# A graph layer on one core: fourteen blocks of nodes gathered, not twelve, through five message tiles

## The chip, the cores and the metric

The kernel runs on one core of a Trainium2 chip. The metric is the device time of one execution in microseconds; lower is better. The kernel before was timed three times: 592.69, 594.62 and 597.58 us, so 594.62 us is its median.

The core's engines work side by side, each on its own queue of instructions, which it takes strictly in order: PE (matrix products), DVE or VectorE, ACT or ScalarE, POOL or GpSimd, and SP, which here only starts transfers. `T`, `V`, `A` and `G` are PE, VectorE, ScalarE and GpSimd in the code.

## The reference

There are 6250 nodes with 128 features each and 100,000 edges, sorted by the node that they point to. An edge has a source, a destination and a type, 0 or 1. The layer computes, for every edge, a linear map of the source's features with the weights of its type, sums these messages at the destination, adds a linear map of the node itself, applies relu, adds the input and normalises each row:

```python
Xs = X[src]
m_data = Xs @ W_data.T + b_data
m_ctrl = Xs @ W_control.T + b_control
msg = jnp.where((edge_types == 0)[:, None], m_data, m_ctrl)
agg = jax.ops.segment_sum(msg, dst, num_segments=X.shape[0])
out = agg + (X @ W_self.T + b_self)
return _layernorm(x + jax.nn.relu(out))
```

The last line joins two lines of the reference. Everything is float32.

## The kernel before

**The table.** The kernel first maps every node with both sets of weights: 49 blocks of 128 nodes, two types, so 98 sub-blocks of 128 rows. Each float32 result is split into three bfloat16 parts that add up to it, so a row has 3 x 128 = 384 numbers. All rows lie in SBUF (`m3`) and also go to DRAM (`table`). The products are `y` at L460 and L462; L478 subtracts the part already taken. The table's stores (L488) are issued by SP.

**A block's edges.** Because edges are sorted, the edges into one block of 128 destinations lie together. The kernel loads for each block a window of 128 x 18 edges (`win` or `win_g`, L372) that covers them. From there, a block takes one of two ways.

**The gathered way** (the last `NG` blocks). For each of a window's 18 columns, POOL starts an indirect transfer that fetches 128 rows of the table from DRAM into a tile `msg` (L854, 98 KB). VectorE writes a matrix of zeros and ones that says which destination each edge has (`hot_g`, L866, six columns at a time), and PE multiplies the two into the sum of the block (`agg_g`). That is 18 steps, and each is four products, since `by_columns` (L232) splits a product into four column pieces of 32 that run side by side. The tiles `msg` are `MB` in number, so gather `i` waits for the product `i - MB` (the step `gm`).

**The packed way** (the first `NPB` blocks). It fetches nothing by row from DRAM. For groups of four or five blocks (`GROUPS`) PE and VectorE sort the edges by the sub-block that their source lies in. Ranking does that: `acc` products with `tri` and `rest` and a reduction `slot` (L563) for each of the 18 columns. The sorted entries are moved to their slots by small products (`small`, L600), written to DRAM (`packed`, L618), and read back spread over all partitions (`rows`, 784 KB for a block, L718). Edges that found no slot go to a list of up to 32, fetched by one indirect transfer per group (`mixed`, L694). Then, for each block, PE picks message rows out of `m3` with `rows` as selecting matrix (`g_ps`, L754, 98 products of 32 rows each, in 25 tiles), ACT copies each tile from PSUM to SBUF (`gs`, L769), and PE adds them up with `hot_d` (L739) into `agg`, four column pieces for each of 25 tiles. In the last group VectorE shares the copies with ACT.

Both ways end alike: the node's own product (`o`), the sum of the three parts (`whole`, L153), relu and residual (L149), the statistics, and once per batch of blocks the normalisation (L168 to L190) and the store. A batch is a group on the packed way, with the last group in two pieces; on the gathered way it is `GQ` blocks.

**What sets the order.** Every part of the work is written as a stream of steps, each with a cost per engine, the steps that it needs, and a due time. A planner (`Order.run`, from L76) takes all streams together and simulates the engines with these costs: it picks the engine that is free first, and of the steps that it could begin, the one with the earliest due time. The order in which it picks them is the order of the instructions in each engine's queue. The costs and due times are numbers in the program, no measurements: `BUILT` is when the table is due, `BLOCK` the time of one packed block, `PACE` that of one gather, `AHEAD` how far ahead of its first block a group's packing is due, and `FIRST` the same for the first group. `PACE` is also the cost of a gather on POOL in the plan, and a gather is planned to land 3.0 us after it starts. On the chip the engines wait for one another by semaphores, so the plan decides the order and not the times.

The part of the plan that the change touches is this:

```python
free = [("gm", *gathered[i - MB])] if i >= MB else [*stored, "idx"]
yield step(("msg", j, k), {"G": PACE}, *free, lag=3.0 - PACE)
msgs[j, k] = late.tile([P, D3], BF16, name="msg", bufs=MB)
```

`stored` are all stores of the table: no gather starts before the whole table is in DRAM.

Of the kernel before, what the change touches and what calls it, by code (L numbers as in the profile page):

```python
# [32 lines left out]
ES = ER // RJ  # L33
EPS = 1e-05

GROUPS = (4,)*2+(5,)*5+(4,)
Q = max(GROUPS)
NPG = len(GROUPS)
NPB = sum(GROUPS)
NG = NB - NPB  # L40
STARTS = [sum(GROUPS[:i]) for i in range(NPG)]
R = 32
# [58 lines left out]
def step(name, costs, *needs, lag=0.0):  # L101
    return as_tuple(name), costs, [as_tuple(n) for n in needs], lag
# [7 lines left out]
def kernel(  # L110
# [95 lines left out]
    with ExitStack() as main:  # L206
        sums_over_windows(main, tc, x, xt, edges, w, bias, table, packed, total,
                          add_parts, finish, load_rows, norm)
# [6 lines left out]
def sums_over_windows(ctx, tc, x, xt, edges, w, bias, table, packed, total,  # L215
# [67 lines left out]
    for j in range(RJ):  # L283
# [17 lines left out]
    counted = {n: const.tile([P, P, n], BF16, name=f"count{n}")  # L301
               for n in sorted({DC, CH, *GROUPS})}
    tri = const.tile([P, P], BF16, name="tri")
# [5 lines left out]
    slot_values = [const.tile([P, (Q + 1) // 2, NT], BF16, name=f"vs{i}") for i in range(2)]  # L309
    slot_b = {n: const.tile([P, R, n], BF16, name=f"slot{n}") for n in sorted({*GROUPS})}  # L310

# [68 lines left out]
                  for g, n in enumerate(PARTS) for b in range(at_part[g], at_part[g] + n, 2)]  # L380


    LEAD, BUILT = 8.0, 78
    BLOCK = 12.9
    PACE = 2.2
    AHEAD, FIRST = 22.0, 14

    def due(kind, *i):
        if kind in ("p", "g") and i[0] in ("root", "rooted", "scale", "apply", "out"):
            n = i[1] + 1  # L390
            return BUILT + 10 + (BLOCK * sum(p[2] for p in PIECES[:n]) if kind == "p" else PACE * KT * GQ * n)
        if kind in ("counted", "turned", "first"):
# [21 lines left out]
        if kind in ("win", "xs", "agg", "o", "whole", "sum"):  # L414
            b = i[0]
            begun = BUILT + (BLOCK * b if b < NPB else PACE * KT * (b - NPB))
            if kind == "win":
                return due("fields", blocks[b][0]) - 8 if b < NPB else BUILT - 20
            if b >= NPB:
                return begun + {"whole": PACE * KT + 2, "sum": PACE * KT + 5}.get(kind, 0)  # L420
            return begun + {"whole": BLOCK + 0.5, "sum": BLOCK + 3}.get(kind, 0.3 * BLOCK)
        if kind in ("rows", "sel", "d", "g", "e", "s"):
            of = {"rows": 1, "sel": 1, "d": 2}.get(kind, NS)
            lead = {"rows": -9, "sel": -3, "d": -1, "g": 0, "e": 1, "s": 2}[kind]
            return BUILT + BLOCK * (i[0] + (i[1] / of if len(i) > 1 else 0)) + lead
        if kind in ("gh", "gm", "msg"):
            k = i[1] * CH if kind == "gh" else i[1]
            return BUILT + PACE * (i[0] * KT + k) + {"msg": 0, "gh": 2, "gm": 5}[kind]
        n = GROUPS[i[0]]
        end = BUILT + BLOCK * STARTS[i[0]] - (AHEAD if i[0] else FIRST)  # L430
        span = BLOCK * n if i[0] else 34.0
        begun = end - span
# [399 lines left out]
    rel_g = const.tile([P, NG, KT], BF16, name="rel_g")  # L832
    msgs, g_hots, kept = {}, {}, []
    GQ = -(-NG // -(-NG // Q))
    MB, XB = 3, 2

    def gathered_fields():
        yield step("idx", {"V": 1.8}, ("y", NB * 3 // 4), *[("win", b) for b in range(NPB, NB)])
# [10 lines left out]
    def gather_rows():  # L849
        for i, (j, k) in enumerate(gathered):  # L850
# [3 lines that stand above are left out]
# [190 lines left out]
```

## Time and profile before

| | before |
|---|---|
| median of three runs | 594.62 us |
| the profiled execution's own time | 628.32 us |
| its span, first to last instruction | 626.6 us |
| PE busy | 554.5 us (88%) |
| ACT busy | 448.4 us (72%) |
| DVE busy | 448.2 us (72%) |
| POOL busy | 255.6 us (41%) |
| moved by DMA | 77.37 MB, 123 GB/s |
| packed blocks, gathered blocks | 37, 12 |

The profile is one execution with the recorder on, and it takes 5.7% longer than the median of the runs without it. Times inside it are set against its own 628.32 us. In it the table is built in the first 75 us or so; then packed and gathered blocks run interleaved until about 603 us, the last gathered block is finished, and the last stores go out. A name such as `g_ps<-m,rows` reads: output tile from input tiles. Matmuls overlap in PE, so the durations of a group add up to more than its busy time. PEld is PE's loading of weights, which runs beside the products.

### The profile page before, as it was taken

To read this page: it belongs to the slowest core of one execution; us is meant where nothing else is said; L and a number is where in the kernel's file an instruction comes from. 1 tells how busy PE (TensorE), PEld (TensorE's weight loads), DVE (VectorE), ACT (ScalarE), POOL (GpSimd) and SP (SyncE) were. 2 spreads that over 40 slices of the span, in tenths; PEclk is the share of its full clock that TensorE was granted. 3 is DMA by queue.
4 is the path that set the end of the run, shared out by engine and by line. 5 is a ranking of instruction groups with operands and counts; after the bars stand their busy time and mean duration, and the time that the engine had idled before them with its cause. 6 is when DMAs were issued, how large, how long until landed. Compare 5 with 4: busy or idle time off the path is not lost.

```text
span 626.6 us, 27468 instructions
## 1 busy us (share of the span) xinstructions
PE 554.5 (88%) x11703; PEld 453.8 (72%) x11703; DVE 448.2 (72%) x1031; ACT 448.4 (72%) x1066; POOL 255.6 (41%) x232
## 2 busy tenths in 40 slices
PE   5899879999999989899999989999998899998950
PEld 3555447887887778787887877788886788777730
DVE  4645687897888786688768876788857766568650
ACT  6756546768877767688678768778787887777631
POOL 1000025544545445545455345455435444444330
PEclk9999989999999999999999999999999999999985
DMA  3669653243434442444324433434424443533120
GB/s 106 187 170 273 203 198 111 53 157 107 136 121 149 118 116 61 153 123 133 106 61 160 125 104 110 146 121 127 129 56 155 135 123 103 158 102 119 45 58 21
DMA packets 59642, 77.37 MB, mean 123 GB/s; under 512 B 15344, under 2 KB 50395, under 8 KB 59511
## 3 DMA queue, kind: packets, MB, share of 16 engines
q1 hardware_dynamic: 47653, 50.56, 25.4%
q0 software_dynamic: 10704, 21.56, 12.5%
q10 hardware_dynamic: 1154, 3.41, 1.8%
q8 instruction: 93, 1.52, 1.0%
q14 instruction: 38, 0.31, 0.2%
HBM read 62.44 MB, written 13.07 MB: 120 GB/s over the span
## 4 chain that ended last, share of the span: by engine, by line
PE 73%; DMA 9%; DVE 5%; issue 5%; ACT 4%; POOL 1%; SPq 1%; another core or an unknown queue 0%; ACTq 0%; POOLq 0%; DVEq 0%
PE agg L232 25%; PE g_ps L754 23%; PE acc L232 8%; DMA msg<-table,idx 7%; PE agg_g L232 6%; PE small L600 5%; PE y L460 3%; ACT gs L769 2%; PE y L478 1%; POOL msg L854 1%; DVE slot L563 1%; ACT h_p L190 1%; DMA rows<-packed 1%; PE y L462 1%; DVE two L584 1%
## 5 line engine op out<-in xcount | busy, mean ns | idle before, releaser
L769 ACT CAST gs<-g_ps 128x384 bf16<-128x384 f32 x856 | 357.8, 494 | 120.8 <-PE g_ps L754 85.7
L754 PE MATMUL g_ps<-m,rows 128*32 128x384 bf16 x3626 | 347.7, 332 | 6.2 <-issue 2.9
L854 POOL DMA_INDIRECT msg<-table,idx x216 | 243.4, 1127 | 263.6 <-PE agg_g L232 122.7
L232 PE MATMUL agg<-gs,hot_d 128*32 128x384 bf16 x3552 | 321.9, 334 | 16.7 <-ACT gs L769 8.2
L232 PEld LDWEIGHTS <-hot_d 128*32 128x32 bf16 x3700 | 212.5, 137 | 47.1 <-issue 36.3
L754 PEld LDWEIGHTS <-rows 128*32 128x32 bf16 x3626 | 201.4, 138 | 31.2 <-issue 25.6
L563 DVE TENSOR_REDUCE slot<-acc 128x5 bf16<-128x490 f32 (+1 forms) x144 | 90.2, 627 | 76.2 <-PE acc L232 49.8
L232 PE MATMUL agg_g<-msg,hot_g 128*32 128x384 bf16 x864 | 93.7, 333 | 13.5 <-DMA msg<-table,idx 11.2
L739 DVE TENSOR_TENSOR hot_d<-count,to 128x1664 bf16<-128x1664 bf16 x74 | 78.7, 1066 | 10.8 <-ACT to L634 5.1
L600 PE MATMUL small<-hot_st,two 128*32 128x98 bf16 x1332 | 66.2, 283 | 2.3 <-DVE ls L684 1.5
L232 PE MATMUL acc<-hot_st,tri 128*32 128x490 bf16 (+1 forms) x576 | 65.4, 359 | 0.2 <-issue 0.2
L232 PE MATMUL acc<-hot_st,rest 128*32 128x490 bf16 (+1 forms) x544 | 60.1, 361 | 6.2 <-DVE slot L563 5.6
L232 PEld LDWEIGHTS <-hot_g 128*32 128x32 bf16 x864 | 46.0, 124 | 19.5 <-issue 18.1
L471 ACT CAST m<-y 128x512 bf16<-128x512 f32 (+1 forms) x75 | 40.9, 580 | 25.9 <-PE y L462 12.8
L600 PEld LDWEIGHTS <-two 128*32 128x32 bf16 x1332 | 53.9, 116 | 6.5 <-issue 2.9
L546 DVE TENSOR_TENSOR hot_st<-count,st_b 128x2940 bf16<-128x2940 bf16 (+1 forms) x24 | 45.0, 1880 | 13.5 <-PE small L600 9.7
L694 POOL DMA_INDIRECT mixed<-table,row_i x8 | 9.9, 1234 | 83.2 <-DVE rows L725 79.0
L725 DVE TENSOR_SCALAR rows<-rows,pid 128x3136 bf16<-128x3136 bf16 x37 | 38.6, 1042 | 2.8 <-DMA rows<-packed 2.3
L460 PE MATMUL y<-w_sb,xt 128*128 128x256 f32 x98 | 34.4, 438 | 1.8 <-DMA xt<-in_xt 1.8
L232 PEld LDWEIGHTS <-rest 128*32 128x32 bf16 x544 | 24.1, 98 | 15.1 <-issue 14.3
L153 DVE TENSOR_REDUCE whole<-agg 128x128 f32<-128x384 f32 x37 | 20.5, 553 | 11.2 <-PE agg L232 5.6
L769 DVE CAST gs<-g_ps 128x384 bf16<-128x384 f32 x32 | 17.2, 555 | 15.2 <-PE g_ps L754 14.4
(140 smaller groups left out, 440.6 us busy)
## 6 DMA issues: line engine op xcount, KB each, us to landing
rows<-packed SPq DMA_DIRECT2D x37, 784.0 KB
table<-m SPq DMA_DIRECT2D x10, 768.0 KB
msg<-table,idx POOLq DMA_INDIRECT x216
xt<-in_xt ACTq DMA_DIRECT2D x5, 512.0 KB
xt_p<-in_xt SPq DMA_DIRECT2D x37, 64.0 KB
xs_p<-in_x SPq DMA_DIRECT2D x37, 64.0 KB
out<-h_p SPq DMA_DIRECT2D x5, 320.0 KB
win<-in_edges SPq DMA_DIRECT2D x37, 27.0 KB
```

Of the source, the lines that this page charges most:

```text
L153: nc.vector.tensor_reduce(whole, agg.rearrange("p (i c) -> p c i", i=3), axis=AX.X, op=ALU.add)
L232: T.matmul(out[c : c + 32], lhsT[:, c : c + 32], rhs, **flags)
L460: T.matmul(y[:, j, :], xts[g][:, b + j - at_part[g], :], w_sb[:, : 2 * D], start=j == 0, stop=False, skip_group_check=True)
L471: A.copy(part_of(b, n, i), ys[b][:, :n, :].rearrange("p b (t c) -> p t b c", t=2))
L546: V.tensor_tensor(hot, counted[n][:, None, 1 : NT + 1, :].to_broadcast([P, KC, NT, n]), fields[grp][2][:, c * KC : c * KC + KC, None, :].t ...
L563: V.tensor_reduce(slots[grp][:, k, :], by_q, axis=AX.X, op=ALU.max)
L600: T.matmul(vt[c0 : c0 + R, q // 2, :], two[:, k % KC, i, :, q], hot[:, k % KC, :, q], start=k == 0 and q < 2, stop=k == KT - 1, skip_group ...
L725: V.tensor_scalar(rows[b], rows[b], pid1, None, op0=ALU.is_equal)
L739: V.tensor_tensor(hot, counted[DC][:, :, :n], places[grp][:, q, None, c * DC : c * DC + n].to_broadcast([P, P, n]), op=ALU.is_equal)
L754: T.matmul(g_ps[t * R : (t + 1) * R, :D3], rows[b][:, :, s], m3[:, s, :], start=True, stop=True)
L769: (A.copy if e == "A" else V.tensor_copy)(gs[at], g_tiles.pop((b, g))[at, :D3])
L854: G.indirect_dma_start(out=msgs[j, k], out_offset=None, in_=table[:, :], in_offset=bass.IndirectOffsetOnAxis(ap=idx[:, j, k : k + 1], axis=0),
```

## The change

Three things change, all of them numbers.

- `GROUPS` goes from two groups of four, five of five and one of four (37 blocks) to seven of five (35 blocks). The number of gathered blocks, `NG`, is what is left of 49: 12 becomes 14, with 18 gathers each, so 216 gathers become 252. `GQ`, the batch of gathered blocks that are normalised together, goes from 4 to 5 by its formula, so the batches are 5, 5 and 4.
- The plan's numbers: `BUILT` 78 to 76, `BLOCK` 12.9 to 13.1, `PACE` 2.2 to 1.75, `AHEAD` 22 to 26, `FIRST` 14 to 20.
- `MB`, the number of tiles for gathered messages, goes from 3 to 5.

```diff
-GROUPS = (4,)*2+(5,)*5+(4,)
+GROUPS = (5,)*7
...
-    LEAD, BUILT = 8.0, 78
-    BLOCK = 12.9
-    PACE = 2.2
-    AHEAD, FIRST = 22.0, 14
+    LEAD, BUILT = 8.0, 76
+    BLOCK = 13.1
+    PACE = 1.75
+    AHEAD, FIRST = 26.0, 20
...
-    MB, XB = 3, 2
+    MB, XB = 5, 2
```

Since the planner orders all queues together, the order of instructions shifts on every engine from the first group on; no instruction of a new kind appears.

## The prediction

> **What bounds the kernel now.** First the page's busy times, with the rows of PE and POOL in the view of the span in 40 slices (one slice is 15.7 us):
>
> ```profile
> PE 554.5 (88%) x11703; PEld 453.8 (72%) x11703; DVE 448.2 (72%) x1031; ACT 448.4 (72%) x1066; POOL 255.6 (41%) x232
> ...
> PE   5899879999999989899999989999998899998950
> ...
> POOL 1000025544545445545455345455435444444330
> ```
>
> PE is at eight tenths or more nearly everywhere between the third slice and the last two; summed in stretches of 20 us from 100 to 600 us its busy time is 93% of the 500 us. No other engine is near that. POOL, which only issues gathers, is half busy. So work taken from PE should count nearly in full, and POOL has room. Next the costliest groups (busy us, mean ns of one, then idle time before them and who ended it):
>
> ```profile
> L769 ACT CAST gs<-g_ps 128x384 bf16<-128x384 f32 x856 | 357.8, 494 | 120.8 <-PE g_ps L754 85.7
> L754 PE MATMUL g_ps<-m,rows 128*32 128x384 bf16 x3626 | 347.7, 332 | 6.2 <-issue 2.9
> L854 POOL DMA_INDIRECT msg<-table,idx x216 | 243.4, 1127 | 263.6 <-PE agg_g L232 122.7
> L232 PE MATMUL agg<-gs,hot_d 128*32 128x384 bf16 x3552 | 321.9, 334 | 16.7 <-ACT gs L769 8.2
> L232 PE MATMUL agg_g<-msg,hot_g 128*32 128x384 bf16 x864 | 93.7, 333 | 13.5 <-DMA msg<-table,idx 11.2
> ```
>
> ACT waits for PE (85.7 us), PE hardly for ACT (8.2 us). POOL stood idle 263.6 us before gathers, because a tile of messages was not free. PE lost 11.2 us waiting for messages to land. The table of waits says it from both ends (us in total, times, longest):
>
> ```profile
> POOL msg L854 <- PE agg_g L232: 122.7, 78, 3.8
> POOL msg L854 <- PE g_ps L754: 107.0, 96, 4.1
> ...
> PE agg_g L232 <- DMA msg<-table,idx: 11.2, 10, 2.4
> ```
>
> Then prices. Matmuls overlap, so their 332 ns are not what one costs PE; the chain that ended last shows the pace at which it advances (start, us, what):
>
> ```profile
> 169.97 0.21 PE acc L232 x4
> 170.17 0.16 PE agg L232 x4
> ...
> 188.67 0.33 PE agg L232 x8
> ```
>
> Four column pieces of 384 take 0.163 us (0.33 over two such fours); four of 490 take 0.21 us. The same chain has 1.84 us for 49 `small` matmuls, 0.0376 us each, and 0.17 us for four `acc` pieces of a group of four (392 wide). Last, the end of the chain:
>
> ```profile
> 601.59 0.75 PE g_ps L754 x2
> ...
> 603.28 0.35 PE agg_g L232 x8
> ...
> 606.23 2.68 DMA msg<-table,idx
> ...
> 608.95 0.60 PE agg_g L232 x3
> ```
>
> The packed work is done at 603.3; the last six steps of the gathered blocks still follow, the last three at the pace of POOL's gathers (603.72, 604.98, 606.23, so 1.26 us apart). The last product ends at 609.55.
>
> **What the Trainium skill says.** "TensorE: Matmul & The Clock Gate", section Back-to-back issue gap, gives an isolated gap of N / 2.4 + 2.5 ns, 162.5 ns for 384 columns and 207 ns for 490; this trace agrees (163 and 210 ns for a four, whose pieces run side by side). "DMA: Bandwidth & Descriptors", section Anatomy of one DMA, fits 2.0 us plus bytes over 436 GB/s to a DMA from GpSimd, for 98 KB an estimate of 2.2 us; the last gather's 2.68 us above, undisturbed by other gathers' waits, is near, while in mid-run the chain shows 4.8 to 7.7 us. "SBUF — State Buffer", its box on how DVE blocks such DMAs, says that descriptor writing stops while VectorE holds the shared port; gathers that took POOL from 0.94 to 2.53 us fit, but no run here isolates it. So landing is a matter of latency, which more tiles in flight cover, unless the transfers themselves are the limit.
>
> **The change part by part.** All in the profile's own time: span 626.6, program 628.32 us; the median of the runs shown is 594.62, a factor of 0.946, by which I scale a difference.
>
> *Two blocks leave the packed path.* Each has 98 `g_ps` and 100 `agg` pieces: 396 pieces, 99 fours at 0.163: -16.1 us of PE. *They join the gathered path*: 2 x 18 fours of `agg_g`: +5.9. Their own-row products (`o`) stay. *Packing* goes from three groups of four and five of five to seven of five. Ranking has 35 fours a group: before 105 x 0.17 + 175 x 0.21 = 54.6, after 245 x 0.21 = 51.5: -3.1. `small` at L600 loses 72 x 0.0376: -2.7. One group's list and position products and two blocks' transposes (L629: 3.5 us for 148) go: about -0.4. Sum on PE: **-16.4 us**, on the path, since PE sets it. That PE's 7% of idle time shrinks with the work would add 1 to 3 us; I take nothing for it and keep 3 for the range.
>
> *Work on engines with room.* ACT loses 50 evictions x 0.42 (357.8 / 856), 21 us; VectorE two `rows` (1.04), four `hot_d` (1.07) and packing, and gains six `hot_g` (0.55): about -10 us net. SP loses two `rows` transfers of 784 KB and one group's stores. POOL gains 36 gathers x 1.127 = 40.6 us and loses one `mixed` (1.2). None counts: PE's queue hides them. Were POOL alone the limit, 252 gathers at the 1.25 us of back-to-back ones are 315 us, well under the 520 from first to last gather. In the last group VectorE shares the evictions over five blocks, not four; also hidden.
>
> *Five tiles.* A gather waits for the product five places back, not three. At before's mean pace, (606.2 - 87.3) / 215 = 2.41 us, three tiles are a ring of 7.2 us, and landings of 4.8 to 7.7 us stall PE. At a needed pace of some 1.95 us (490 / 252) five tiles are a ring of 9.8 us. Three at that pace would be 5.9 us, so the closer pace needs the tiles. PE's waits for messages are 11.2 us, of which 2.28 + 0.76 + 0.73 = 3.8 at the end; from the 7.4 in mid-run I take back **3 us** (bounds: none, as landings lengthen, and all 7.4). What is late next there is PE's wait for evictions (8.2 us), which is small.
>
> *The end.* In the instruction order of the changed program PE's last gathered four stands 6.5 fours of `g_ps` and 10 of `agg` ahead of its end (2.7 us), where before six gathered fours followed all else. The run then ends with the last packed block, which before had finished at 603.3, against 609.55: **-6 us** (bounds 0, if PE waits for messages there as before, and -7). The last gathered batch stays four blocks (batches of 5, 5, 4), and its 5 us of normalising run beside the last products.
>
> *The start.* The first group has five blocks: in the order, PE's work ahead of the first `g_ps` (a `y` product by the chain at 0.43, 0.21 and 0.11 us for L460, L462 and L478) is 59.8 us against 58.3 (inside the sum above). But the first group's transposes now stand 6.7 us of work ahead of the last table product, not 0.7 us; before, the last `y` ended at 73.8 and the first `g_ps` began only at 82.6, behind VectorE's list and select. That may give up to 4 us. Against it: SP's queue now has the first group's stores and three `rows` spreads ahead of the last four table stores, where one pair of stores was ahead of all of that and two spreads stood ahead of the last pair. One more 784 KB at the 220 GB/s of 60 to 80 us is 3.6 us later for the table and so for the first gather (before at 87.3); PE comes to its first message 10.2 us of work after the first `g_ps` instead of 6.7, which covers that. I take 0, bounds -4 and +5.
>
> *Plan numbers* (`BUILT`, `BLOCK`, `PACE`, `AHEAD`, `FIRST`) only reorder the queues; no wait is added. A message not landed holds everything behind it on PE: `g_ps`, then ACT's evictions. `XB` stays 2; a chunk of hots lasts six steps, 11.7 us, so its 0.55 us stays hidden.
>
> Sum: -16.4 - 3 - 6 + 0 = -25.4: 628.3 becomes 602.9, and x 0.946 is **570.5 us**.
>
> **The rivals.** *PE work only*: landings lengthen with five in flight, and the end keeps a wait. Then only -16.4 stays: 611.9, or 579. For it: waits for messages came in bursts in mid-run; against: POOL's stalls were for tiles. *Slower: gathers set the pace.* If before's spacing was the transfers' own and not the three tiles', 36 more gathers lengthen the run. The point is a mean pace of (609.55 - 87.3) / 252 = 2.07 us; at 2.15 the last gather lands near 629, 20 us late: about 648, or 613. For it: landings of up to 7.7 us and the mean of 2.41. Against: POOL waited on PE in 174 of the spaced gathers, and the last ones landed 1.26 us apart. *It does little*: later table stores hold PE at its first message and new in-order stalls cost 20 us more: about 589 to 600; the 3.6 us above speaks against that much. *More*: idle shrinks with the work, all mid-run waits go, and the start gains 4: -37, some 560.
>
> **How the numbers follow.** Forecast (562 to 577) 0.60; PE only (577 to 588) 0.20; more (under 562) 0.07; little (589 to 600) 0.06; slower 0.07. About 1%, 6 us, is what a measurement of this kernel can tell from no change. The range of 560 to 588 leaves out the little and slower cases and the far end of the best. Faster 0.87, same 0.06, slower 0.07.
>
> **What would show it.** Right: 3430 `g_ps`, 1008 `agg_g` pieces; PE busy near 538; POOL's idle before gathers down by more than half of 263.6; mean gather spacing near 1.95 us; PE's wait for messages under 8 us; the chain ending in `h_p` or only just in `h_g`, with no string of message waits at the end. Wrong: message waits above 15 us on PE, a mean spacing over 2.07 us, or a first `g_ps` later than 87 us.

## The result and the profile after

The changed kernel takes 547.74 us, the median of four runs (545.63 to 548.73). Four runs of the kernel before, on the same chip, have a median of 593.65 us (590.95 to 597.58). The ratio is 0.9217, with a 95% interval of 0.9157 to 0.9277, so the change saves 46 us. The forecast was 570.5 us, a saving of 24. The direction was right; the time lies 12 us below the low end of the range.

One fact has to come first, because the comparisons below depend on it. The experiments ran on five chips, each in one session, and the kernel before falls into one of two groups by chip. On chips 1, 8 and 14 its median is 592 to 597 us, as in the result above. On chips 13 and 15 the very same program takes 626 us, and no session mixes the two. As each chip had one session only, "chip" here may stand for something else that was the same throughout it. The profile that the prediction was read from took 628.32 us itself, beside runs of 592.69 to 597.58 us, so it looks like an execution of the second group (no chip is recorded with it). Below, "595-us chip" and "626-us chip" name the two groups, and every ratio is to the kernel before on the same chip. The ratios leave out runs that lie more than 1.5% above the fastest of the same kernel.

The busy times of the changed kernel, and the rows of PE and POOL in the view of the span in 40 slices (13.6 us each):

```profile
span 543.9 us, 26402 instructions
...
PE 504.0 (93%) x11222; PEld 440.7 (81%) x11222; DVE 425.9 (78%) x958; ACT 422.6 (78%) x1012; POOL 296.4 (54%) x267
...
PE   4899978999899999999999999999999999979990
...
POOL 1000004776766667767487576676677556676610
```

The profiled execution took 545.63 us, one of the four runs of the median, with no 5.7% on top. PE was busy 504.0 us where I had foreseen about 538, from a profile in which the kernel before has 554.5; on chip 1 it has 528.2. From the twelfth slice to the 35th every digit of PE is 9. The costliest groups, and the waits (total us, times, longest):

```profile
L769 ACT CAST gs<-g_ps 128x384 bf16<-128x384 f32 x807 | 334.3, 495 | 71.3 <-PE g_ps L754 58.2
L854 POOL DMA_INDIRECT msg<-table,idx x252 | 285.9, 1135 | 133.7 <-PE g_ps L754 64.9
L754 PE MATMUL g_ps<-m,rows 128*32 128x384 bf16 x3430 | 319.1, 331 | 0.0
L232 PE MATMUL agg_g<-msg,hot_g 128*32 128x384 bf16 x1008 | 108.0, 329 | 7.2 <-DMA msg<-table,idx 6.8
```

```profile
POOL msg L854 <- PE g_ps L754: 64.9, 121, 2.6
...
POOL msg L854 <- PE agg_g L232: 50.3, 75, 2.7
...
PE agg_g L232 <- DMA msg<-table,idx: 6.8, 8, 1.6
```

The counts are the foreseen ones. POOL's idle time before gathers fell from 263.6 us in the first profile (230.8 on chip 1) to 133.7, and PE waits 6.8 us for messages. The gathers start from 89.0 to 520.4 us, so their mean spacing is 431.4 / 251 = 1.72 us, where before it was 2.41. The end of the chain (start, us, what):

```profile
530.36 1.02 PE agg L232 x14
531.38 0.54 DVE whole L153
...
533.04 1.65 ACT h_g L190 x4
...
535.97 0.49 ACT h_p L190
```

The last product belongs to a packed block, at 531.4 us; the last product of messages began at 527.3. There is no string of waits for messages at the end, and `h_p` is the last to be normalised.

### The profile page after: what moved, and what is told of

It is laid out like the page before. It is cut to its first block, busy times and chain, and to the rows that moved or that the text cites. A ratio compares the mean times of both kernels' runs of the same rounds, so it can differ in the third digit from the quotient of the medians.

```text
span 543.9 us, 26402 instructions
## 1 busy us (share of the span) xinstructions
PE 504.0 (93%) x11222; PEld 440.7 (81%) x11222; DVE 425.9 (78%) x958; ACT 422.6 (78%) x1012; POOL 296.4 (54%) x267
## 4 chain that ended last, share of the span: by engine, by line
PE 72%; DMA 11%; DVE 9%; ACT 3%; issue 2%; SPq 1%; POOL 1%; DVEq 0%; ACTq 0%; POOLq 0%
PE agg L232 23%; PE g_ps L754 22%; PE acc L232 8%; PE small L600 7%; PE agg_g L232 7%; DMA msg<-table,idx 5%; DMA rows<-packed 5%; PE y L460 2%; DVE hot_st L546 2%; DVE slot L563 1%; ACT gs L769 1%; ACT h_p L190 1%; PE y L478 1%; DVE rows L725 1%; ACT h_g L190 1%
## 5 line engine op out<-in xcount | busy, mean ns | idle before, releaser
L769 ACT CAST gs<-g_ps 128x384 bf16<-128x384 f32 x807 | 334.3, 495 | 71.3 <-PE g_ps L754 58.2
L854 POOL DMA_INDIRECT msg<-table,idx x252 | 285.9, 1135 | 133.7 <-PE g_ps L754 64.9
L754 PE MATMUL g_ps<-m,rows 128*32 128x384 bf16 x3430 | 319.1, 331 | 0.0
L232 PE MATMUL agg<-gs,hot_d 128*32 128x384 bf16 x3360 | 298.2, 329 | 3.7 <-ACT gs L769 3.2
L232 PEld LDWEIGHTS <-hot_d 128*32 128x32 bf16 x3500 | 188.8, 137 | 11.4 <-issue 6.8
L232 PE MATMUL agg_g<-msg,hot_g 128*32 128x384 bf16 x1008 | 108.0, 329 | 7.2 <-DMA msg<-table,idx 6.8
L563 DVE TENSOR_REDUCE slot<-acc 128x5 bf16<-128x490 f32 x126 | 83.5, 663 | 36.3 <-PE acc L232 28.3
L232 PE MATMUL acc<-hot_st,rest 128*32 128x490 bf16 x476 | 54.4, 376 | 7.9 <-DVE slot L563 7.8
L232 PE MATMUL acc<-hot_st,tri 128*32 128x490 bf16 x504 | 60.5, 375 | 1.1 <-DVE hot_st L546 1.1
L694 POOL DMA_INDIRECT mixed<-table,row_i x7 | 8.2, 1169 | 86.5 <-PE g_ps L754 80.5
L546 DVE TENSOR_TENSOR hot_st<-count,st_b 128x2940 bf16<-128x2940 bf16 x21 | 41.9, 1999 | 7.7 <-PE small L600 6.3
L153 DVE TENSOR_REDUCE whole<-agg 128x128 f32<-128x384 f32 x35 | 19.3, 552 | 12.3 <-PE agg L232 9.2
L769 DVE CAST gs<-g_ps 128x384 bf16<-128x384 f32 x33 | 18.0, 555 | 12.9 <-PE g_ps L754 12.4
```

Of the source, the lines that this page charges most:

```text
L153: nc.vector.tensor_reduce(whole, agg.rearrange("p (i c) -> p c i", i=3), axis=AX.X, op=ALU.add)
L232: T.matmul(out[c : c + 32], lhsT[:, c : c + 32], rhs, **flags)
L546: V.tensor_tensor(hot, counted[n][:, None, 1 : NT + 1, :].to_broadcast([P, KC, NT, n]), fields[grp][2][:, c * KC : c * KC + KC, None, :].t ...
L563: V.tensor_reduce(slots[grp][:, k, :], by_q, axis=AX.X, op=ALU.max)
L754: T.matmul(g_ps[t * R : (t + 1) * R, :D3], rows[b][:, :, s], m3[:, s, :], start=True, stop=True)
L769: (A.copy if e == "A" else V.tensor_copy)(gs[at], g_tiles.pop((b, g))[at, :D3])
```

## The experiments

The theories have letters, and the expectations use them. **A**: the ring of three message tiles cost PE far more than the 11.2 us that the profile before names. **B**: it cost what that profile names, and the rest comes from the new order. **C**: the gain beyond the tiles comes from the plan's numbers. **D**: a plan in which the gathers end long before the packed work fills PE badly. **E**: the next bound is the pace of POOL or of the transfers, near 1.5 us. **F**: on a 626-us chip PE has stalls of its own, which the tiles do not touch.

### The parts one by one, on chip 14

The kernel before takes 596.74 us here. The first kernel keeps before's order of instructions on every engine and gives the messages five tiles. The planner still believes in three, because only the pool's size is changed:

```diff
-            msgs[j, k] = late.tile([P, D3], BF16, name="msg", bufs=MB)
+            msgs[j, k] = late.tile([P, D3], BF16, name="msg", bufs=5)
```

> The kernel before with every instruction in the order that it had, and five tiles behind msg where it had three. Theory A (the ring of three tiles cost PE far more than the 11.2 us that the profile names, since a late message also holds the copies and the weight loads behind it): 20 to 30 us faster, 565 to 575 us, PE's idle time before weight loads falls by half. Theory B (the ring costs what the profile names, the rest of the gain is the new plan of the order): 3 to 7 us faster, 587 to 591.

The second is its mirror image, the changed kernel's order with three tiles:

```diff
-            msgs[j, k] = late.tile([P, D3], BF16, name="msg", bufs=MB)
+            msgs[j, k] = late.tile([P, D3], BF16, name="msg", bufs=3)
```

> The changed kernel with every instruction in its order, but three tiles behind msg. Theory A: the gain goes, 575 to 600 us, mean gather spacing over 1.9 us and messages late on PE by 20 us or more in all. Theory B: 551 to 556 us, a loss of 4 to 8 us.

The third and fourth take one part each, the groups or the plan's numbers, with three tiles:

```diff
-GROUPS = (4,)*2+(5,)*5+(4,)
+GROUPS = (5,)*7
```

> The kernel before with seven groups of five, so fourteen gathered blocks, its old plan numbers and three tiles. PE has 16.4 us less to do by the prediction's prices. Theory A: the ring of three tiles has 36 more gathers to serve at 2.2 us of plan, which ends them after the packed work: no gain or slower, 590 to 610. Theory B: about 16 us faster, 577 to 582.

```diff
-    LEAD, BUILT = 8.0, 78
-    BLOCK = 12.9
-    PACE = 2.2
-    AHEAD, FIRST = 22.0, 14
+    LEAD, BUILT = 8.0, 76
+    BLOCK = 13.1
+    PACE = 1.75
+    AHEAD, FIRST = 26.0, 20
```

> The kernel before with the new plan numbers (BUILT, BLOCK, PACE, AHEAD, FIRST) only: 37 packed blocks, three tiles. Theory A: the closer pace asks three tiles for what they cannot give, so within 5 us of before or slower, 589 to 610. Theory B: 10 to 20 us faster, 574 to 584, from the earlier start and the gathers that end before the packed work.

| part of the change | us | ratio to before (95%) | PE's wait for messages, us |
|---|---|---|---|
| before's order, five tiles | 569.69 | 0.956 (0.950 to 0.962) | 5.1 |
| the new order, three tiles | 609.59 | 1.022 (1.014 to 1.031) | 61.2 |
| groups alone, three tiles | 628.51 | 1.055 (1.050 to 1.061) | 53.7 |
| plan's numbers alone, three tiles | 629.76 | 1.053 (1.044 to 1.062) | 48.6 |

The 609.59 us is the middle of 606.47 and 612.71; the other two runs of that kernel took 628.63 and 615.75 us, and the last is the profiled one. Five tiles alone, in an unchanged order, save 27.0 us. Everything else without them makes the kernel slower by 2 to 5%, and PE waits 49 to 61 us for messages. The table of waits of the new order with three tiles:

```profile
PEld L232 <- issue: 97.5, 108, 4.7
...
PE agg_g L232 <- DMA msg<-table,idx: 61.2, 52, 4.5
```

The changed kernel has 6.8 us there, in the same order with two tiles more. This speaks for A in its direction, and it shows that the closer pace needs the tiles. The sizes are beyond A: it gave the three kernels without the tiles at most 600, 610 and 610 us. But 27 us is more than the 11.2 us of the profile before, all of it; why is answered below by a profile of before taken on a 595-us chip.

### The parts in pairs and a step further, on chip 13

Here the kernel before was also run by itself once more:

> The kernel before, unchanged. Its first profile took 628.32 us, 33 us over its median, while the changed kernel's profile took what its median says. If recording slows a kernel whose queue waits on three tiles, this profile takes 615 us or more again; if that execution was an odd one, 590 to 602.

Then the changed kernel with the old groups (12 gathered blocks), and with the old plan's numbers:

```diff
-GROUPS = (5,)*7
+GROUPS = (4,)*2+(5,)*5+(4,)
```

> Five tiles and the new plan numbers, but the old groups (37 packed blocks, 12 gathered). Theory A (with the ring gone, PE's work sets the time): the two blocks are worth the 16.4 us of PE's priced work, so 561 to 567 us. Rival C (the gain past the five tiles is the plan numbers'): 548 to 555. Rival D (gathers planned at 1.75 end far ahead of 37 packed blocks, so PE is less well filled late): 568 to 580.

```diff
-    LEAD, BUILT = 8.0, 76
-    BLOCK = 13.1
-    PACE = 1.75
-    AHEAD, FIRST = 26.0, 20
+    LEAD, BUILT = 8.0, 78
+    BLOCK = 12.9
+    PACE = 2.2
+    AHEAD, FIRST = 22.0, 14
```

> Five tiles and seven groups of five, but the old plan numbers, so gathers planned 2.2 us apart: 252 of them end about 554 in the plan, after the packed work at 78 + 35 x 12.9 = 530. Theory A: the two blocks' work goes from PE, but the last gathered blocks are left alone at the end: 560 to 575 us. Rival C: like the same-order run with five tiles, 566 to 572, as only the plan numbers would help. Were the plan numbers worth nothing: 546 to 552.

And a step further on the same way, with 17 blocks gathered:

```diff
-GROUPS = (5,)*7
+GROUPS = (5,)*4+(4,)*3
...
-    PACE = 1.75
+    PACE = 1.35
...
-    MB, XB = 5, 2
+    MB, XB = 7, 2
```

> Beyond the change: 17 gathered blocks, 32 packed (four groups of five, three of four), gathers planned at 1.35 us, seven tiles. Theory A: three packed blocks less are 3 x 8.1 = 24 us less on PE, and 306 gathers at the 1.25 us of back-to-back ones are 383 us, still under PE's time: 520 to 532 us. Rival E (POOL's or the transfers' pace is reached near 1.5 us): 306 x 1.5 = 459 us from about 88 us on, 555 to 570.

The kernel before took 626.1 us here, in its single run, which was profiled, as in the others (median 626.29), so it is not recording that makes it slow. All three kernels were slower than it: 646.59 us (ratio 1.034), 660.56 us (1.054) and 688.09 us (1.099). No theory had foreseen that. Either the pairs of parts are bad, or this chip is different. The profile of before on this chip has

```profile
PE agg_g L232 <- DMA msg<-table,idx: 12.8, 13, 1.8
```

which is close to the 11.2 us of the profile that the prediction was read from.

### The same kernels on chip 15

To tell these apart, two kernels whose times on a 595-us chip were known went to a chip together with two of those just run:

> The changed kernel, unchanged, to see how its gain stands on the chip that this group of runs falls on: the kernel before took 594 to 597 us in some groups of runs and 626 us in another. Where before takes about 595: 545 to 550 us. Where it takes about 626: theory F (PE stalls of half a microsecond there that the tiles do not touch): 590 to 620 us; theory A alone: the same 8% as before, 572 to 582.

> The kernel before with its order kept and five tiles, once more. Where before takes about 595: 567 to 573 us. Where it takes about 626: by theory A 4 to 5% faster, 594 to 602; by theory F (the tiles are not what holds PE there) within 2%, 614 to 632.

> Five tiles and the new plan numbers with the old groups, once more. Where before takes about 595: by theory A the two blocks are worth PE's 16.4 us, so 561 to 567 us; by rival D (a plan whose gathers end far ahead of 37 packed blocks fills PE badly late) 568 to 585. Where it takes about 626: 644 to 649 as measured there.

> Five tiles and seven groups of five with the old plan numbers, once more. Where before takes about 595: the gathers planned 2.2 us apart end after the packed work, so the last gathered blocks are alone: 570 to 600 us; if the plan numbers are worth nothing, 546 to 552. Where it takes about 626: 659 to 662 as measured there.

Chip 15 is a 626-us chip too: before takes 626.56 us (one of its seven runs took 2807.16). The changed kernel takes 632.99 us (ratio 1.013, 1.010 to 1.016), before's order with five tiles 636.09 us (1.015, 1.012 to 1.018), the old groups 645.1 us and the old plan 660.25 us, within 1.5 us of chip 13. **On this chip the change saves nothing: the kernel is 1.3% slower with it.** The verdict turns with the chip, and so does that of its main part, the tiles. F had given 590 to 620 us for the changed kernel and 614 to 632 for the five tiles, so even F was too hopeful. What differs there is told in the last section.

### The kernel before and the pairs, on chip 1

What was still open was how large the message waits of before are on a 595-us chip, and what the pairs of parts do there:

> The kernel before, unchanged, for its profile. On the chip where it takes about 595 us, theory A has PE waiting 30 us or more for messages in this profile (11.2 us in the first profile, 5.1 us in the same-order run with five tiles), and fewer of the stalls before weight loads than the 72.7 us of the first profile. On the 626 us chip: 11 to 14 us of message waits again.

> Five tiles and the new plan numbers, old groups. Where before takes about 595: 561 to 567 us if two blocks are worth PE's 16.4 us on top of the change's 547.7; 568 to 585 if the plan suits 37 packed blocks badly. Where it takes 626: 644 to 648.

> Five tiles and seven groups of five, old plan numbers. Where before takes about 595: 570 to 600 us, with the last gathered blocks alone at the end and PE idle there; 546 to 552 if the plan numbers are worth nothing. Where it takes 626: 659 to 662.

> 17 gathered blocks, seven tiles, gathers planned at 1.35 us. Where before takes about 595: theory A gives 520 to 535 us (24 us less of PE's work than the change); if gathers meet a pace of their own near 1.5 us, 550 to 570. Where it takes 626: 683 to 691.

The kernel before takes 592.52 us on chip 1, and its profiled execution 599.19. Its waits, beside those of before's order with five tiles (chip 14) in the second fence:

```profile
POOL msg L854 <- PE agg_g L232: 98.6, 88, 3.5
...
PEld L232 <- issue: 62.6, 90, 3.7
...
PE agg_g L232 <- DMA msg<-table,idx: 32.4, 24, 3.5
...
PEld L754 <- issue: 8.6, 37, 0.3
```

```profile
POOL msg L854 <- PE agg_g L232: 77.8, 72, 3.0
...
PEld L232 <- issue: 31.0, 74, 1.9
PEld L754 <- issue: 12.0, 46, 1.0
...
PE agg_g L232 <- DMA msg<-table,idx: 5.1, 5, 1.6
```

On this 595-us chip PE waits 32.4 us for messages, not 11.2. Five tiles bring this to 5.1 us: 27.3 us less, and the two medians on chip 14 lie 27.05 us apart. The chain that ended last says it too (share of the span by line; first before on chip 1, then its order with five tiles on chip 14):

```profile
PE agg L232 19%; DMA msg<-table,idx 18%; PE g_ps L754 17%; PE acc L232 7%; PE agg_g L232 5%; PE small L600 4%; PE y L460 3%; POOL msg L854 3%; DMA rows<-packed 2%; ACT gs L769 1%; PE y L478 1%; ACT h_p L190 1%; DVE slot L563 1%; PE y L462 1%; SPq L368 1%
```

```profile
PE agg L232 26%; PE g_ps L754 25%; PE acc L232 10%; PE small L600 7%; PE agg_g L232 6%; PE y L460 3%; ACT gs L769 2%; DMA msg<-table,idx 2%; PE y L478 1%; DVE hot_st L546 1%; DVE slot L563 1%; ACT h_p L190 1%; DMA rows<-packed 1%; DVE rows L725 1%; PE y L462 1%
```

Landing messages are 18% of the span in the chain of before, 2% with five tiles, and were 7% in the profile that I had. So A holds in its size, and B holds in its reading: the ring costs what a profile in the same condition names, and the copies and weight loads behind a late message need not be added.

The pairs, with five tiles, give 573.95 us for the old groups (ratio 0.965, 0.957 to 0.973) and 606.52 us for the old plan (1.022, 1.015 to 1.030). With the old plan's numbers and the new groups, 252 gathers are planned 2.2 us apart. They follow each other at 2.14 us, (526.5 - 92.1) / 203, while there is packed work, and 48 of them are left when it ends. Two rows by tile (the last two of the times are the first and last start):

```profile
L754 PE MATMUL g_ps<-m,rows x3430: 322/326/535, 85.4 to 526.6; 128*32 128x384 bf16 x191
```

```profile
L232 PE MATMUL agg_g<-msg,hot_g x1008: 323/326/528, 95.9 to 589.7; 128*32 128x384 bf16 x168
```

Packed work ends at 527, and PE then takes gathered steps alone for 63 us, with a gather every 1.25 us. This has the outcome of the rival in which gathers set the pace, but not its cause: the spacing was the plan's and not the transfers' own. With the old numbers 14 blocks cost 59 us more (606.52 against 547.74, or 60 by the ratios), more than the 570 to 600 us that was expected.

With the old groups and the new numbers it is the other way round: the last of 216 gathers starts at 463.4, and the packed work goes on without them. That kernel is 26 us slower than the changed one, more than the 16.4 us of work in two blocks, and its time lies in D's range. But the stretch after the gathers does not show a badly filled PE (from, to, length, then busy us and count of PE, PEld, DVE, ACT and POOL, clock, DMA share, GB/s):

```profile
472.00:552.00 80.00, 76.46 (x1793) 66.31 (x1787) 58.98 (x143) 71.60 (x181) 0.88 (x1) 1.00 0.23 76
```

PE is busy 76.46 of these 80 us. Over the whole span its busy time is 21.9 us more than the changed kernel's (525.9 against 504.0), and 4.6 us more pass after the last product. So D's reason is not shown, and why two blocks cost more than 16.4 us here stays open. C is too simple: with the old groups and five tiles the new numbers gain nothing (0.965, against 0.956 with the old numbers), and with the new groups they gain 59 us. They pay only with the groups that they belong to.

Seventeen gathered blocks give 559.24 us (0.943, 0.936 to 0.951), faster than before and slower than fourteen. Its waits:

```profile
POOL msg L854 <- PE g_ps L754: 45.7, 150, 0.3
...
PE agg_g L232 <- DMA msg<-table,idx: 35.7, 30, 2.7
```

150 of POOL's waits add up to 45.7 us and none is longer than 0.3. The gathers follow each other at 1.25 us in the median and 1.45 on average, (535.7 - 94.3) / 305, so POOL issues them nearly one after another, and PE waits for messages all the same. The time lies in E's range of 550 to 570 us and not in A's of 520 to 535, so a bound of E's kind is met with 17 blocks; whether it is POOL's pace or the transfers' is not separated. With 14 there is still room.

### Between fourteen and seventeen, on chip 8

Fifteen gathered blocks with seven tiles, and the changed kernel's own order with eight:

```diff
-GROUPS = (5,)*7
+GROUPS = (5,)*6+(4,)
...
-    PACE = 1.75
+    PACE = 1.6
...
-    MB, XB = 5, 2
+    MB, XB = 7, 2
```

> 15 gathered blocks, 34 packed (six groups of five, one of four), gathers planned at 1.6 us, seven tiles. Where before takes about 594: one packed block less is 8 us of PE's work, 539 to 545 us, since 270 gathers at 1.6 us are 432 us, still inside PE's time; 548 to 560 if messages hold PE already. Where it takes 626: slower than before by 2 to 5%, as with 17 blocks it was by 10%.

```diff
-            msgs[j, k] = late.tile([P, D3], BF16, name="msg", bufs=MB)
+            msgs[j, k] = late.tile([P, D3], BF16, name="msg", bufs=8)
```

> The changed kernel, every instruction in its order, eight tiles behind msg for five. Where before takes about 594: at most the 6.8 us of message waits in its profile, 541 to 548 us. Where it takes 626: 626 to 640, as more tiles bring nothing there.

Before takes 595.55 us (587.95 to 602.93). Eight tiles give 544.69 us (0.918, 0.910 to 0.927), where five gave 0.922, so more than five bring nothing that shows: PE's waits for messages are 4.1 us, from 6.8. Fifteen blocks give 541.33 us (0.913, 0.903 to 0.923), the fastest of all. It beats both kernels in its median, but its interval overlaps that of the changed kernel, and the two were not run side by side. That fifteen is better than fourteen is therefore not shown.

## Why the prediction was right or wrong

**What failed is the term for five tiles**, as the prediction put it: PE's waits for messages are 11.2 us, "from the 7.4 in mid-run I take back 3 us (bounds: none, as landings lengthen, and all 7.4)". It measured 27 us, in time and in the wait lines alike, with the order of instructions held. The mechanism was right in that PE waits for messages which a ring of three tiles lets start too late; the size was not. Even its upper bound was too low, for it was taken from one profile that fits a 626-us chip. There PE itself runs slower, and gathers follow each other at 2.41 us on average, where on chip 1 it is 2.28; the message waits are 11.2 and 32.4 us. That PE comes to its messages later there, and so finds more of them landed, fits this but was not tested.

The landings of 4.8 to 7.7 us that the prediction set against the ring were not typical: they were read from the chain, which passes through the late ones. Over all 216 gathers of that profile the time from issue to the last data packet is 2.6 us in the median, 4.2 at the 90th percentile and 5.9 at most. On chip 1 it is 2.7, 4.6 and 6.2 us, and 89 of the 216 take longer than the 3.0 us that the plan gives a gather. So by these figures it is the slow part of the landings that the ring has to cover. They did not lengthen with five in flight: in all kernels with three or five tiles, on both kinds of chip, the median is 2.4 to 3.0 us.

**The scaling by 0.946 failed as a reading.** I took the gap between the profile's 628.32 us and the median of 594.62 for the cost of recording and scaled all savings down by it. Profiled executions elsewhere took no such extra: 545.63 us beside a median of 547.74, 599.19 beside 592.52, 626.1 beside 626.29. The gap was most likely between chips: the kernel before, profiled on chip 13, has the time and the message waits of that first profile. I could have seen it as a question: none of my steps says what those 34 us were, and the waits that a faster PE would meet were not in the profile.

**PE's work, -16.4 us, fits, but no run isolates it.** In before's order with five tiles the packed work ends at 547.5, in the changed kernel at 531.4: 16.1 us earlier, in spans on two 595-us chips. The plan's numbers change in this step too. PE's busy time fell by more, from 525.3 to 504.0. With five tiles and the new plan in both, the old groups end their last product at 555.1, 23.7 us later than the new ones. So the price of the two blocks may be too low.

**The end, -6 us, held in sign.** In before's order with five tiles one wait for a message of 2.69 us is left at the end, and the last product ends at 551.4, 3.9 us after the packed work. In the changed kernel packed work ends last. Moreover, the time from the last product to the end of the span is 17.0 us there and 12.5 in the changed kernel: 4.5 us that I had not counted. They do not come from the block that ends the run. The old groups with the new plan also end in one packed block, as the changed kernel does, and take 17.1 us; the new groups with the old plan end in a gathered batch, as before does, and take 12.3. So this time goes with the groups, and its cause is open. Together 8.4. Tiles apart, the sum was -22.4 us, and the medians differ by 569.69 - 547.74 = 22.0 us (20 by the two ratios). That they meet so closely is in part luck, since 4.5 us of it was in no term.

**The start, 0, was about right.** The first `g_ps` starts at 79.9 us, from 82.4 in the first profile and 81.6 on chip 1, and the first gather at 89.0, from 87.3 and 86.5: both shifts lie within the bounds of -4 and +5.

**The rivals.** "More", at 560 us and 0.07, was the nearest one, yet it too was built on 11.2 us of message waits. "Gathers set the pace" did not come true with the change, since the mean spacing is 1.72 us and not over 2.07. "PE work only" falls with the five-tile run, and "it does little" with the result itself.

**The signs.** The counts, PE's 6.8 us of message waits and a chain that ends in `h_p` came as foreseen. The mean spacing is 1.72 us and not near 1.95, PE's busy time 504.0 and not near 538, and POOL's idle time before gathers fell by 49% of 263.6 us and not by more than half. The last two were set against a profile that was most likely of the other kind of chip.

**The limit of this explanation.** It holds for the 595-us chips. On a 626-us chip, from which the profile most likely came, the same steps would have foreseen 602.9 us, and the kernel takes 633. There the forecast would have failed in its sign.

## What to carry to other kernels

A ring of buffers is to be judged by what it costs when its consumer runs without other stalls: here the two profiles of the 626-us kind showed 11.2 and 12.8 us of waits where the ring cost 27 elsewhere, which fits a consumer that comes too late to wait. A closer pace of transfers, the buffers that it needs and the plan that places it pay together only; here each of the groups and the plan alone with the old ring was 5% slower, and both together 2%. When a profile's own time and the median of the runs differ by more than the runs do among each other, the profile may be of another condition, and its waits are to be measured again there before they are priced.

## What the runs showed of the hardware

The same program takes 570 us on chip 14 and 636 us on chip 15 (before's order with five tiles). Single instructions last equally long: the median `g_ps` product is 326 ns in both groups, and landings are alike. What grows is time between the products. Part of it shows as idle time of PE and PEld for which the profile names no wait (`issue`). Part of it is in PE's busy time, 564.2 us against 525.3 for the same number of products, equally long, so they overlap less. The waits of that kernel on chip 15, where chip 14 had 31.0, 12.0 and 5.1 us in the three lines of PE and PEld (`remote` is a queue or core that the profile does not tell):

```profile
PEld L232 <- issue: 69.6, 148, 1.9
...
PEld L754 <- issue: 30.9, 89, 1.2
...
ACT gs L769 <- remote: 10.0, 5, 3.9
...
PE agg_g L232 <- DMA msg<-table,idx: 2.2, 2, 1.7
```

Adding up the two lines of the weight load that end in "issue" and taking off the waits for messages, which seem to show in them as well, leaves an estimate of 38 to 39 us in before on chip 1, in its order with five tiles on chip 14 and in the changed kernel, and at most 56 in any kernel on these chips. On the 626-us chips it leaves 82 us for before, 98 for its order with five tiles, 118 for the changed kernel and 169 for seventeen gathered blocks. There the change loses what it gains. The stall is largest where the gathers are closest (1.86 us apart with seventeen blocks, 2.05 in the changed kernel), but closeness alone is not the cause: with five tiles in before's order they are 2.45 us apart, against 2.40 with three, and the stall still grew from 82 to 98. A stretch of PE's timeline on chip 15 (start, us, what, idle time before it):

```profile
413.90 0.30 PE L232 MATMUL agg<-w_sb,xt_p 128*32 128x128 f32 x2 [0.39 <-issue]
414.62 0.27 PE L232 MATMUL agg<-w_sb,xt_p 128*32 128x128 f32 x1 [0.42 <-issue]
415.33 0.28 PE L232 MATMUL agg<-bias,ones_b 128*32 128x128 bf16 x4 [0.44 <-issue]
416.05 0.55 PE L232 MATMUL agg<-gs,hot_d 128*32 128x384 bf16 x6 [0.44 <-issue]
```

PE starts again every 0.72 us, with no wait that the profile shows. Between 100 and 500 us PE ran fewer products per time there (in the order of the columns: from, to, length, then busy us and count of PE, PEld, DVE, ACT and POOL, clock, DMA share, GB/s); the first fence is chip 14, the second chip 15:

```profile
100.00:500.00 400.00, 393.16 (x9600) 358.00 (x9593) 339.26 (x758) 342.29 (x850) 216.53 (x187) 1.00 0.44 131
```

```profile
100.00:500.00 400.00, 376.52 (x8457) 318.83 (x8448) 308.39 (x678) 302.92 (x746) 193.43 (x168) 1.00 0.38 116
```

9600 products against 8457 in the same 400 us, at the same granted clock of 1.00. This supports F in kind: the tiles do not take these stalls away. The granted clock, equal in both, does not explain them. What does (the chip, where the memory lies, or something else) stays open, and no run tried to take it away.
